# Softplus slices held back around each Silu slice, and the unit behind a Silu computed with both C products on VectorE

## The chip, the cores and the metric

The kernel runs on one NeuronCore of a Trainium2 chip. The metric is the device time of one execution in microseconds; lower is better. All arithmetic is in float32. The engines are named as the profile names them: PE is TensorE (PEld its weight load), DVE is VectorE, ACT is ScalarE, POOL is GpSimd and SP is SyncE, whose queue issues the DMAs.

## The reference, cut to what matters

The program is two residual blocks on 16 images of 64 x 64 pixels with 96 channels. The first block upsamples, applies two small matrix products with a square between them, and filters down again. The second is a state-space block (a "Mamba" block in four directions):

```
xz = x @ in_proj_w.T;  xc, z = halves of xz;  z = silu(z)
xc = silu(conv3x3_depthwise(xc) + conv_b)             # 192 channels
for each of 4 directions k:                           # rows, columns, both reversed
    dts, Bs, Cs = split(x_proj_weight[k] @ xs[k])     # 6 + 16 + 16 rows
    delta = softplus(dt_projs_weight[k] @ dts + bias)
    h[t] = exp(delta[t] * A) * h[t-1] + (delta[t] * u[t]) * B[t]   # 192 x 16 states
    y[t] = sum over the 16 states of h[t] * C[t]
y = layernorm(sum of the 4 directions) * z;  out = x + y @ out_proj_w.T
```

Each block has a group normalisation ahead of it. There are 64 x 64 = 4096 steps t for each image and direction.

## The kernel before, in words

**The scan and its units.** The scan over t dominates. It is cut into *units*: 128 partitions hold 32 channels times 4 states, and a unit covers two such groups (e = 1 and e = 0) over T = 1024 steps. For an image there are 8 *steps* (two pairs of directions, four lengths of 1024), in each step 6 blocks of channels, and in each block 4 units (j = 0 to 3, four states each). That makes 24 units in a step, 192 in an image and 3072 in all. The loop `for n, (st, bi, j) in enumerate(units)` writes out by hand the order in which every engine gets its instructions. In unit n stand, in this order:

- DVE scans group e = 1 (`recur`, lines 770 and 772, a TENSOR_TENSOR_SCAN of 128 x 1024). It reads the decay `da` (in PSUM, two buffers) and the drive `b` (in SBUF, four buffers).
- The product of h with C for e = 1 goes to POOL (line 915), or in every fifth unit (`odd_here`, SHARE = 5) to DVE (line 906). I call a unit of the second kind *odd*. In an odd unit the scan's result stays in `da`; otherwise it is written over `b`.
- `keep` (line 778) copies the last state for the next step, on DVE or, in odd units and for e = 0, on ACT.
- `decay(n + 1, 1)` (line 755) makes exp(delta * A) of the next unit on ACT. Then comes `slot(0)`.
- POOL multiplies `drive(n + 2)` (line 761, 128 x 2048).
- DVE scans e = 0, PE adds up unit n - 1 (`read_out`, line 794), then `slot(1)`; DVE multiplies with C (line 924), ACT keeps the state and makes `decay(n + 1, 0)`; every fourth unit, at j = 0, ACT copies the finished sums out (`store`, yt, line 805). Last comes `slot(2)`.

**The background work.** All else of the program is woven into those three slots of a unit. It is written as Python generators that yield after each *slice*, and `slot` lets them go on when they are due:

- `project` computes delta, delta * u, B and C for the coming step. It has 71 slices for the 72 slots of a step. For each of 6 pieces it does on ACT the softplus as Abs and Exp (lines 674, 675), Relu and Identity (677, 678), Ln and Identity (680, 681), a slice each; then PE adds the four parts in PSUM (line 686, "4 matmuls"), and three slots later DVE makes dtu (line 691) and ACT copies delta (692).
- `front` is the first block and the convolution of the next image. Its convolution has 12 tiles (8 and 4) in an image. A tile takes four slices: three with a third of the taps each on PE (line 482, the last with z_ps), and then, after `yield WAIT`, the *Silu slice*: a table load, Silu of the convolution (line 500), Silu of z (501), and the load of the usual table (502). `turn` copies the tile column-wise on ACT (line 467) and issues its stores on SP; it stands in the first slice of the next tile.
- `finish` is the end of the image before: the sum of directions, the normalisation and the output product.

`Background` counts a generator's slices against slots passed: 550 weighted slices of `front` over the 576 slots of an image, where a HEAVY slice counts twice. A slice behind `yield WAIT` goes only into slot 2. `front` and then `finish` share one place in a slot; `project` has its own. In each of the images 0 to 14 the Silu slices fall into units 99 to 128 of 192 (in the order before: 99, 102, 104, 107, 109, 112, 114, 116, 121, 123, 126, 128); the last image has no next one to prepare.

**What orders it.** Each engine takes its instructions in the order written; waits follow from the data and from the buffers' reuse. The slot's code before is this:

```
def slot(position):
    step_gen.slot(position)
    (ahead_gen if ahead_gen.gen is not None else behind_gen).slot(position)
...
odd_here = n % SHARE == SHARE - 1
```

Of the kernel before, what the change touches and what calls it, by code (L numbers as in the profile page):

```python
# [70 lines left out]
POS = 3 * 8 * 6 * NQ  # L71
SLICES = 550
WAIT = -1
HEAVY = 2
PSLICES = 71
SHARE = 5
# [3 lines left out]
def tile_two_blocks(  # L80
# [159 lines left out]
    def front(mi):  # L240
# [220 lines left out]
        for i, n, tiles, both in ((0, 128, 8, 0), (1, 64, 4, 4)):  # L461
            col = b16.tile([128, tiles * TB], F32, name="col", tag="b16")
            halves = [(n * k, t0) for k, t0 in enumerate((0, both)[:128 // n])]
            turned = None

            def turn(t, row, z):
                nc.scalar.copy(
                    col.rearrange("c (w h) -> c w h", w=HW)[:, :, 8 * t:8 * t + 8],
                    row.rearrange("c (h w) -> c w h", w=HW),
                )  # L470
                for p, t0 in halves:
                    cols = slice(TB * (t + t0), TB * (t + t0) + TB)
                    nc.sync.dma_start(out=made["xs"][2 * i, 0:n, cols], in_=row[p:p + n])
                    nc.sync.dma_start(out=made["z"][128 * i:128 * i + n, cols], in_=z[p:p + n])

            for t in range(tiles):
                c_ps = bank([128, 8, HW], "c_ps")
                for tap in range(9):
                    dy, dx = divmod(tap, 3)
                    for p, t0 in halves:  # L480
                        h0 = 8 * (t + t0) + dy
                        nc.tensor.matmul(  # L482
                            c_ps[p:p + n], lhsT=wtap_s[:, tap, 128 * i:128 * i + n],
                            rhs=xgp[:, h0:h0 + 8, dx:dx + HW], start=(tap == 0), stop=(tap == 8),
                            skip_group_check=True,
                        )
                    if tap == 2 and turned is not None:
                        turn(*turned)
                    if tap % 3 == 2 and tap < 8:
                        yield HEAVY  # L490
                z_ps = bank([128, 8, HW], "z_ps")
                for p, t0 in halves:
                    h0 = 8 * (t + t0) + 1
                    nc.tensor.matmul(
                        z_ps[p:p + n], lhsT=zwt_s[:, 128 * i:128 * i + n], rhs=xgp[:, h0:h0 + 8, 1:HW + 1],
                        start=True, stop=True, skip_group_check=True,
                    )
                yield WAIT
                row, z = piece([128, TB], "row"), piece([128, TB], "z")
                nc.scalar.activation(row, c_ps.rearrange("c h w -> c (h w)"), AF.Silu, bias=convb_s[:, i:i + 1])  # L500
                nc.scalar.activation(z, z_ps.rearrange("c h w -> c (h w)"), AF.Silu)
                nc.scalar.preload_act_table_set(BOTH)
                turned = t, row, z
                yield HEAVY
            turn(*turned)
            yield HEAVY
            if i == 0:
                yield from parts(made["xs"][1], col)
            else:
                for p, t0 in halves:  # L510
                    to = made["xs"][2, 64:128, :].rearrange("c (w h) -> c w h", h=HW)
                    for w0 in range(0, HW, 16):
                        nc.sync.dma_start(
                            out=to[:, w0:w0 + 16, 8 * t0:8 * t0 + 32],
                            in_=col[p:p + n].rearrange("c (w h) -> c w h", w=HW)[:, w0:w0 + 16, :],
                        )
                        yield HEAVY

# [96 lines left out]
    def scan():  # L615


        with ExitStack() as es:
# [14 lines left out]
            def project(mi, pair, lc, out):  # L633
# [17 lines left out]
                for t in range(0, T, TB):  # L651
                    u, ahead_u = dict(zip(order, ahead_u)), []
                    pp = gps.tile([128, TB], F32, name="pp", tag="g")
                    for v in range(3):
                        nc.tensor.matmul(pp, lhsT=xpt_s[:, pair, v, :], rhs=u[v], start=(v == 0), stop=(v == 2))
                    for _ in range(2):
                        yield
                    pr = pj.tile([128, TB], F32, name="pr")
                    nc.scalar.activation(pr, pp, AF.Identity, bias=bumps_s)


                    for i, v in enumerate(order):
                        if i == 0:
                            yield
                        s = gps.tile([128, TB], F32, name="s", tag="g")
                        nc.tensor.matmul(s, lhsT=dtw_s[:, pair, v, :], rhs=pr, start=True, stop=True)  # L666
                        if i == 0:
                            for r in range(2):
                                nc.sync.dma_start(
                                    out=rows[r, :, t:t + TB], in_=pr[64 * r:64 * r + 2 * NS, :]  # L670
                                )
                        yield
                        e, d, m, w = (pj.tile([128, TB], F32, name=k) for k in ("e", "d", "m", "w"))
                        nc.scalar.activation(e, s, AF.Abs)
                        nc.scalar.activation(e, e, AF.Exp, scale=-1.0)
                        yield
                        nc.scalar.activation(m, s, AF.Relu)
                        nc.scalar.activation(w, e, AF.Identity, bias=one_s)
                        yield
                        nc.scalar.activation(d, e, AF.Ln, bias=one_s)  # L680
                        nc.scalar.activation(w, w, AF.Identity, scale=-1.0, bias=one_s)  # L681
                        yield
                        s = gps.tile([128, TB], F32, name="s", tag="g")
                        yield
                        for k, of in enumerate((w, e, d, m)):
                            nc.tensor.matmul(s, lhsT=ident_s, rhs=of, start=(k == 0), stop=(k == 3))  # L686
                        for _ in range(3):
                            yield
                        dtu = pj.tile([128, TB], F32, name="dtu")
                        delta = pj.tile([128, TB], F32, name="delta")  # L690
                        nc.vector.tensor_mul(dtu, s, u[v])
                        nc.scalar.copy(delta, s)  # L692
                        for _ in range(2):
                            yield
                        nc.sync.dma_start(out=out["dtu"][v][:, t:t + TB], in_=dtu)
                        nc.sync.dma_start(out=out["delta"][v][:, t:t + TB], in_=delta)
                        if t + TB < T and i < 2:
                            ahead_u += [fetch_u(k, t + TB) for k in (order[:1], order[1:])[i]]
# [123 lines left out]
            class Background:  # L822

                def __init__(self, gen, slices, positions):
                    self.gen, self.slices, self.positions, self.at, self.n = gen, slices, positions, 0, 0
                    self.wait = False

                def slot(self, position):  # L830
                    self.at += 1
                    if self.wait and position < 2:
                        return
                    if self.gen is not None and self.n * self.positions < self.at * self.slices:
                        self.step()

                def step(self):
                    weight = next(self.gen, 0)
                    if weight == 0:
                        self.gen = None  # L840
                    else:
                        self.wait = weight == WAIT
                        self.n += 1 if weight in (None, WAIT) else weight

                def drain(self):
                    while self.gen is not None:
# [1 line left out]

            nothing = Background(None, 0, 1)
            ahead_gen = behind_gen = step_gen = nothing  # L850

            def slot(position):
                step_gen.slot(position)
                (ahead_gen if ahead_gen.gen is not None else behind_gen).slot(position)

            last = len(units) - 1
            def next_step(st, mi):
# [9 lines left out]
                drive(n)  # L867
            for e in range(2):
                decay(0, e)
            storing = None  # L870

            for n, (st, bi, j) in enumerate(units):
                mi, pair, lc = steps[st]
# [2 lines left out]
                if n % per_image == 0:  # L876
                    image[mi]["y"] = dram.tile([2, DI, L], F32, name="y_d")
                    behind_gen.drain()
                    ahead_gen = behind_gen = nothing
# [19 lines left out]
                    if ahead:  # L899
                        deltas[m + 1, 1] = fetch_delta(*ahead, 1)  # L900

                odd_here = n % SHARE == SHARE - 1
# [157 lines left out]
```

## Time and profile before

| what | value |
|---|---|
| median of 3 runs | 21502.07 us (21501.11 to 21510.08) |
| profiled execution, its own time | 21508.85 us |
| its span | 21507.1 us |
| DVE busy | 19512.2 us, 91% |
| POOL busy | 19511.8 us, 91% |
| PE busy | 16918.9 us, 79% |
| ACT busy | 13741.5 us, 64% |
| first scan to last scan | 536 to 21340 us |
| one image (mean of images 0 to 14) | 1304.9 us |

Times from the profile are of that one execution. A line such as "L770 DVE TENSOR_TENSOR_SCAN" names the source line, the engine and the operation; behind it stand what is written and read, how often, the busy time, the mean of one in ns, and the engine's idle time ahead of these instructions with what ended it. Where I give a figure by unit, I took the starts of the e = 1 scans (every second start of lines 770 and 772) as the units' bounds, put each instruction and the idle time just before it into the unit in which it starts, and averaged over images 0 to 14.

### The profile page before, as it was taken

The page shows a single profiled execution, that of the slowest core. Times are in us where ns is not written, and L with a number is a line of the kernel's source. Part 1 is how long each engine was busy: PE and PEld are TensorE (multiplying, and loading weights), DVE is VectorE, ACT ScalarE, POOL GpSimd, SP SyncE. Part 2 cuts the span into 40 slices and gives each one's busy share as a digit, 9 for nine tenths or more (in the row PEclk, how much of TensorE's full clock was granted, in tenths as well). Part 3 has the DMA queues.
Part 4 walks back from the last instruction along what each step waited for, and adds up shares of the span by engine and source line. Part 5 has one row for each costly group of instructions (what it writes and reads, how often), then busy time and mean ns, then how long its engine had stood idle before and what let it go on. Part 6 is the DMA issues. An engine that isn't in the chain of part 4 may idle for free. (4 is left out here: it accounts for less than half of the span.)

```text
span 21507.1 us, 273615 instructions
## 1 busy us (share of the span) xinstructions
PE 16918.9 (79%) x98988; PEld 7271.3 (34%) x98988; DVE 19512.2 (91%) x12983; ACT 13741.5 (64%) x20546; POOL 19511.8 (91%) x5538
## 2 busy tenths in 40 slices
PE   7776877878878788787878778788787888878855
PEld 4423324233332333324333242333423333243221
DVE  0999999999999999999999999999999999999997
ACT  3666666667666666666666666676666666666553
POOL 0999999999999999999999999999999999999996
PEclk8887888888889888898888888888898888888877
DMA  2565565656656566565655656566565665656654
GB/s 74 180 207 184 199 224 187 217 192 204 217 189 227 187 218 203 187 228 183 219 197 200 224 191 215 192 208 215 185 227 187 211 203 192 230 184 217 222 186 140
DMA packets 1855466, 4277.13 MB, mean 199 GB/s; under 512 B 449438, under 2 KB 548670, under 8 KB 1852062
## 3 DMA queue, kind: packets, MB, share of 16 engines
q1 hardware_dynamic: 1854110, 4259.62, 58.8%
q8 instruction: 781, 12.80, 0.2%
q14 instruction: 575, 4.71, 0.1%
HBM read 3380.58 MB, written 878.18 MB: 198 GB/s over the span
## 5 line engine op out<-in xcount | busy, mean ns | idle before, releaser
L761 POOL TENSOR_TENSOR b<-dtu,bt 128x2048 f32<-128x2048 f32 x3072 | 13905.1, 4536 | 594.2 <-DMA dtu<-dtu_d 530.5
L755 ACT ACTIVATE da<-delta,a_s 128x1024 f32<-128x1024 f32 x6144 | 6852.3, 1116 | 2859.4 <-DVE b L924 888.2
L915 POOL TENSOR_TENSOR b<-b,ct 128x1024 f32<-128x1024 f32 x2458 | 5804.1, 2361 | 1235.6 <-DVE new L778 832.6
L794 PE MATMUL y<-b,fold_s 128*32 128x256 f32 x49152 | 3837.1, 435 | 1111.6 <-DVE b L924 551.4
L924 DVE TENSOR_TENSOR b<-da,ct 128x1024 f32<-128x1024 f32 x3072 | 3756.5, 1223 | 93.9
L770 DVE TENSOR_TENSOR_SCAN da<-da,new,b 128x1024 f32<-128x1024 f32 x1383 | 3246.5, 2347 | 282.8 <-ACT da L755 274.7
L772 DVE TENSOR_TENSOR_SCAN da<-da,new,b 128x1024 f32<-128x1024 f32 x1382 | 3242.4, 2346 | 125.5 <-ACT da L755 119.1
L794 PEld LDWEIGHTS y<-b,fold_s 128*32 128x32 f32 x49152 | 1392.0, 119 | 3857.0 <-issue 1333.0
L778 ACT COPY new<-da 128x1 f32<-128x1 f32 x2764 | 434.6, 157 | 2786.4 <-DVE b L924 2294.7
L772 DVE TENSOR_TENSOR_SCAN b<-da,new,b 128x1024 f32<-128x1024 f32 x922 | 2157.9, 2341 | 47.0 <-ACT da L755 46.1
L770 DVE TENSOR_TENSOR_SCAN b<-da,new,b 128x1024 f32<-128x1024 f32 x921 | 2156.6, 2342 | 41.1 <-ACT da L755 39.5
L482 PE MATMUL c_ps<-xgp,wtap_s 96*128 96x512 f32 (+1 forms) x4608 | 1721.3, 642 | 203.6 <-ACT row L500 199.1
L686 PE MATMUL s<-w,ident_s 128*128 128x512 f32 x1536 | 1175.4, 857 | 872.0 <-ACT w L681 752.3
L666 PE MATMUL s<-pr,dtw_s 128*128 128x512 f32 x1536 | 939.0, 696 | 544.6 <-ACT delta L692 328.0
L365 PE MATMUL h_ps<-xu,w1t_s 96*128 96x500 f32 x1920 | 1059.4, 652 | 306.7 <-ACT hsq L348 124.2
L377 PE MATMUL o_ps<-w2c_s,hsq 128*100 128x96 f32 x9600 | 1031.9, 266 | 170.0 <-ACT hsq L348 143.7
L772 DVE TENSOR_TENSOR_SCAN da<-da,b 128x1024 f32<-128x1024 f32 x461 | 1055.9, 2291 | 118.4 <-ACT da L755 116.7
L770 DVE TENSOR_TENSOR_SCAN da<-da,b 128x1024 f32<-128x1024 f32 x460 | 1053.4, 2290 | 106.5 <-ACT da L755 104.3
L377 PEld LDWEIGHTS o_ps<-w2c_s,hsq 128*100 128x100 f32 x9600 | 966.1, 178 | 357.2 <-ACT hsq L348 184.9
L686 PE MATMUL s<-e,ident_s 128*128 128x512 f32 x1536 | 1022.9, 755 | 0.0
L482 PEld LDWEIGHTS c_ps<-xgp,wtap_s 96*128 96x128 f32 (+1 forms) x4608 | 600.1, 172 | 1154.9 <-issue 873.0
L787 PE MATMUL y<-y,ident_s 128*128 128x512 f32 x768 | 534.1, 784 | 538.6 <-ACT yt L805 537.1
(128 smaller groups left out, 21920.7 us busy)
## 6 DMA issues: line engine op xcount, KB each, us to landing
dtu<-dtu_d SPq DMA_DIRECT2D x1536, 512.0 KB
delta<-delta_d SPq DMA_DIRECT2D x1536, 512.0 KB
bt<-rows SPq DMA_DIRECT2D x1024, 512.0 KB
ct<-rows SPq DMA_DIRECT2D x1024, 512.0 KB
u<-xs_d SPq DMA_DIRECT2D x896, 256.0 KB
dtu_d<-dtu SPq DMA_DIRECT2D x768, 256.0 KB
delta_d<-delta SPq DMA_DIRECT2D x768, 256.0 KB
xr<-in_x SPq DMA_DIRECT2D x768, 128.0 KB
```

Source lines behind the costliest of these rows:

```text
L365: nc.tensor.matmul(h_ps[j], lhsT=w1t_s[:, 128 * j:128 * (j + 1)], rhs=xu.rearrange("c p q -> c (p q)"), start=True, stop=True,)
L377: nc.tensor.matmul(o_ps[:, p, :], lhsT=hsq[j][:, UPS * p:UPS * (p + 1)], rhs=w2c_s[:, j, :], start=(j == 0), stop=(j == HB - 1),)
L482: nc.tensor.matmul(c_ps[p:p + n], lhsT=wtap_s[:, tap, 128 * i:128 * i + n], rhs=xgp[:, h0:h0 + 8, dx:dx + HW], start=(tap == 0), stop=(tap ...
L666: nc.tensor.matmul(s, lhsT=dtw_s[:, pair, v, :], rhs=pr, start=True, stop=True)
L686: nc.tensor.matmul(s, lhsT=ident_s, rhs=of, start=(k == 0), stop=(k == 3))
L755: nc.scalar.activation(da, deltas[n // NQ, e], AF.Exp, scale=a_s[:, k, g, units[n][2]:units[n][2] + 1])
L761: nc.gpsimd.tensor_mul(b, dtus[n // NQ], bt.unsqueeze(1).to_broadcast([128, 2, T]))
L770: nc.vector.tensor_tensor_scan(out, da, b, before, ALU.mult, ALU.add)
L772: nc.vector.tensor_tensor_scan(out[:, ::-1], da[:, ::-1], b[:, ::-1], before, ALU.mult, ALU.add)
L794: nc.tensor.matmul(y[32 * q:32 * q + 32, e, :], lhsT=fold_s, rhs=b[:, e, QT * q:QT * q + QT], start=(pair == 0 and j == 0 and e == 0), sto ...
L915: nc.gpsimd.tensor_mul(h, h, bc[1, r, j])
L924: nc.vector.tensor_mul(bs[n][:, 0, :], h, bc[1, r, j])
```

## The change

A slice of `project` can now be announced as BUSY: `yield BUSY` says that the next slice is one of softplus (or the input copy pr, or dtu and delta), which load ACT. `slot` decides for both generators. When the Silu slice is due, in slot 2 and with no `store` under way (so not at j = 0), it sets `full = 2`: in this slot and the next, BUSY slices of `project` are left out. They are made up for later: where `project` lags and its slice is a light one, it may take a second light one in the same slot. The unit behind a Silu slice (`full_unit`) becomes an odd one. A running `credit` keeps the share of odd units at one in five: each odd unit takes five credits, also where it comes early, and after a run of early ones none follow until the credit is back at five. And `turn` moves from the first slice of the next tile (tap 2) to the second (tap 5).

With that, units 99 to 130 of an image get 12 or 13 odd units (6 or 7 before), and the next one comes between units 160 and 164. The numbers of instructions of each kind that compute stay the same.

```
--- before.py
+++ after.py
@@ -71,6 +71,7 @@
 POS = 3 * 8 * 6 * NQ
 SLICES = 550
 WAIT = -1
+BUSY = -2
 HEAVY = 2
 PSLICES = 71
 SHARE = 5
@@ -484,7 +485,7 @@
                             rhs=xgp[:, h0:h0 + 8, dx:dx + HW], start=(tap == 0), stop=(tap == 8),
                             skip_group_check=True,
                         )
-                    if tap == 2 and turned is not None:
+                    if tap == 5 and turned is not None:
                         turn(*turned)
                     if tap % 3 == 2 and tap < 8:
                         yield HEAVY
@@ -653,8 +654,8 @@
                     pp = gps.tile([128, TB], F32, name="pp", tag="g")
                     for v in range(3):
                         nc.tensor.matmul(pp, lhsT=xpt_s[:, pair, v, :], rhs=u[v], start=(v == 0), stop=(v == 2))
-                    for _ in range(2):
-                        yield
+                    yield
+                    yield BUSY
                     pr = pj.tile([128, TB], F32, name="pr")
                     nc.scalar.activation(pr, pp, AF.Identity, bias=bumps_s)
 
@@ -669,14 +670,14 @@
                                 nc.sync.dma_start(
                                     out=rows[r, :, t:t + TB], in_=pr[64 * r:64 * r + 2 * NS, :]
                                 )
-                        yield
+                        yield BUSY
                         e, d, m, w = (pj.tile([128, TB], F32, name=k) for k in ("e", "d", "m", "w"))
                         nc.scalar.activation(e, s, AF.Abs)
                         nc.scalar.activation(e, e, AF.Exp, scale=-1.0)
-                        yield
+                        yield BUSY
                         nc.scalar.activation(m, s, AF.Relu)
                         nc.scalar.activation(w, e, AF.Identity, bias=one_s)
-                        yield
+                        yield BUSY
                         nc.scalar.activation(d, e, AF.Ln, bias=one_s)
                         nc.scalar.activation(w, w, AF.Identity, scale=-1.0, bias=one_s)
                         yield
@@ -684,8 +685,9 @@
                         yield
                         for k, of in enumerate((w, e, d, m)):
                             nc.tensor.matmul(s, lhsT=ident_s, rhs=of, start=(k == 0), stop=(k == 3))
-                        for _ in range(3):
+                        for _ in range(2):
                             yield
+                        yield BUSY
                         dtu = pj.tile([128, TB], F32, name="dtu")
                         delta = pj.tile([128, TB], F32, name="delta")
                         nc.vector.tensor_mul(dtu, s, u[v])
@@ -823,24 +825,20 @@
 
 
 
+
                 def __init__(self, gen, slices, positions):
                     self.gen, self.slices, self.positions, self.at, self.n = gen, slices, positions, 0, 0
-                    self.wait = False
-
-                def slot(self, position):
-                    self.at += 1
-                    if self.wait and position < 2:
-                        return
-                    if self.gen is not None and self.n * self.positions < self.at * self.slices:
-                        self.step()
+                    self.said = None
+
+                def due(self):
+                    return self.gen is not None and self.n * self.positions < self.at * self.slices
 
                 def step(self):
-                    weight = next(self.gen, 0)
-                    if weight == 0:
+                    self.said = next(self.gen, 0)
+                    if self.said == 0:
                         self.gen = None
                     else:
-                        self.wait = weight == WAIT
-                        self.n += 1 if weight in (None, WAIT) else weight
+                        self.n += self.said if self.said is not None and self.said > 0 else 1
 
                 def drain(self):
                     while self.gen is not None:
@@ -848,10 +846,25 @@
 
             nothing = Background(None, 0, 1)
             ahead_gen = behind_gen = step_gen = nothing
+            full, full_unit = 0, None
 
             def slot(position):
-                step_gen.slot(position)
-                (ahead_gen if ahead_gen.gen is not None else behind_gen).slot(position)
+                nonlocal full, full_unit
+                back = ahead_gen if ahead_gen.gen is not None else behind_gen
+                back.at += 1
+                step_gen.at += 1
+                gate = back.said == WAIT and back.due() and position == 2 and storing is None
+                if gate:
+                    full, full_unit = 2, n + 1
+                if step_gen.due() and not (full and step_gen.said == BUSY):
+                    light = step_gen.said != BUSY
+                    step_gen.step()
+
+                    if light and step_gen.due() and step_gen.said != BUSY:
+                        step_gen.step()
+                if back.due() and (gate or back.said != WAIT):
+                    back.step()
+                full = max(full - 1, 0)
 
             last = len(units) - 1
             def next_step(st, mi):
@@ -867,7 +880,7 @@
                 drive(n)
             for e in range(2):
                 decay(0, e)
-            storing = None
+            storing, credit = None, 0
 
             for n, (st, bi, j) in enumerate(units):
                 mi, pair, lc = steps[st]
@@ -899,7 +912,11 @@
                     if ahead:
                         deltas[m + 1, 1] = fetch_delta(*ahead, 1)
 
-                odd_here = n % SHARE == SHARE - 1
+
+                credit += 1
+                odd_here = n == full_unit or credit >= SHARE
+                if odd_here:
+                    credit -= SHARE
                 h = das[n, 1] if odd_here else bs[n][:, 1, :]
                 recur(n, 1, h)
                 if odd_here:
```

More of the change, by code (lines that the diff above doesn't have):

```diff
@@ L73 @@
 WAIT = -1
+BUSY = -2
 HEAVY = 2
@@ L486, in front @@
                         )
-                    if tap == 2 and turned is not None:
+                    if tap == 5 and turned is not None:
                         turn(*turned)
@@ L655, in project @@
                         nc.tensor.matmul(pp, lhsT=xpt_s[:, pair, v, :], rhs=u[v], start=(v == 0), stop=(v == 2))
-                    for _ in range(2):
-                        yield
+                    yield
+                    yield BUSY
                     pr = pj.tile([128, TB], F32, name="pr")
@@ L671, in project @@
                                 )
-                        yield
+                        yield BUSY
                         e, d, m, w = (pj.tile([128, TB], F32, name=k) for k in ("e", "d", "m", "w"))
@@ L675, in project @@
                         nc.scalar.activation(e, e, AF.Exp, scale=-1.0)
-                        yield
+                        yield BUSY
                         nc.scalar.activation(m, s, AF.Relu)
                         nc.scalar.activation(w, e, AF.Identity, bias=one_s)
-                        yield
+                        yield BUSY
                         nc.scalar.activation(d, e, AF.Ln, bias=one_s)
@@ L686, in project @@
                             nc.tensor.matmul(s, lhsT=ident_s, rhs=of, start=(k == 0), stop=(k == 3))
-                        for _ in range(3):
+                        for _ in range(2):
                             yield
+                        yield BUSY
                         dtu = pj.tile([128, TB], F32, name="dtu")
@@ L827, in __init__, with due @@
                     self.gen, self.slices, self.positions, self.at, self.n = gen, slices, positions, 0, 0
[L828 to L835, printed above, removed]
+                    self.said = None
+                def due(self):
+                    return self.gen is not None and self.n * self.positions < self.at * self.slices
                 def step(self):
-                    weight = next(self.gen, 0)
-                    if weight == 0:
+                    self.said = next(self.gen, 0)
+                    if self.said == 0:
                         self.gen = None
                     else:
-                        self.wait = weight == WAIT
-                        self.n += 1 if weight in (None, WAIT) else weight
+                        self.n += self.said if self.said is not None and self.said > 0 else 1
                 def drain(self):
@@ L850, in scan @@
             ahead_gen = behind_gen = step_gen = nothing
+            full, full_unit = 0, None
             def slot(position):
-                step_gen.slot(position)
-                (ahead_gen if ahead_gen.gen is not None else behind_gen).slot(position)
+                nonlocal full, full_unit
+                back = ahead_gen if ahead_gen.gen is not None else behind_gen
+                back.at += 1
+                step_gen.at += 1
+                gate = back.said == WAIT and back.due() and position == 2 and storing is None
+                if gate:
+                    full, full_unit = 2, n + 1
+                if step_gen.due() and not (full and step_gen.said == BUSY):
+                    light = step_gen.said != BUSY
+                    step_gen.step()
+                    if light and step_gen.due() and step_gen.said != BUSY:
+                        step_gen.step()
+                if back.due() and (gate or back.said != WAIT):
+                    back.step()
+                full = max(full - 1, 0)
             last = len(units) - 1
@@ L869, in scan @@
                 decay(0, e)
-            storing = None
+            storing, credit = None, 0
             for n, (st, bi, j) in enumerate(units):
@@ L900, in scan @@
                         deltas[m + 1, 1] = fetch_delta(*ahead, 1)
-                odd_here = n % SHARE == SHARE - 1
+                credit += 1
+                odd_here = n == full_unit or credit >= SHARE
+                if odd_here:
+                    credit -= SHARE
                 h = das[n, 1] if odd_here else bs[n][:, 1, :]
```

## The prediction

> **What bounds the kernel now.** I read the page's busy totals first, then the groups, then busy time by stretch, then the waits of the worst stretch, last its timeline.
>
> ```profile
> PE 16918.9 (79%) x98988; PEld 7271.3 (34%) x98988; DVE 19512.2 (91%) x12983; ACT 13741.5 (64%) x20546; POOL 19511.8 (91%) x5538
> ```
>
> VectorE (DVE) and GpSimd (POOL) are equally busy; ScalarE (ACT) is not the bound on average. The groups that set the two:
>
> ```profile
> L761 POOL TENSOR_TENSOR b<-dtu,bt 128x2048 f32<-128x2048 f32 x3072 | 13905.1, 4536 | 594.2 <-DMA dtu<-dtu_d 530.5
> ...
> L915 POOL TENSOR_TENSOR b<-b,ct 128x1024 f32<-128x1024 f32 x2458 | 5804.1, 2361 | 1235.6 <-DVE new L778 832.6
> ...
> L924 DVE TENSOR_TENSOR b<-da,ct 128x1024 f32<-128x1024 f32 x3072 | 3756.5, 1223 | 93.9
> ```
>
> I call a unit odd when VectorE takes both products with C. Per unit POOL does 4.54 us (L761), and 2.36 (L915) unless odd; back to back the starts of two L761 stand 6.80 apart (POOL's timeline, 10682.65 to 10696.25, two pairs). DVE does two scans (2.3 each), L924 (1.22), a small copy; an odd unit adds L906 (1.225) and drops the copy (0.155): **+1.07 us**. So five units need about 32 us of either.
>
> A unit starts at its first scan, so the starts of L770/L772 cut each image into 192 units. Image 7 of 0 to 15: units 0-98, 99-130 (the Silu stretch), 131-163, 164-191, and for comparison 99-130 of image 15, which has no next image to prepare:
>
> ```profile
> 9664.80:10343.20 678.40, 512.68 (x3778) 264.43 (x3778) 631.55 (x411) 449.74 (x721) 630.82 (x180) 0.83 0.56 190
> 10343.20:10572.10 228.90, 200.31 (x934) 74.39 (x934) 200.01 (x138) 172.47 (x233) 205.17 (x58) 0.93 0.59 204
> 10572.10:10793.20 221.10, 184.41 (x792) 61.41 (x796) 214.19 (x155) 128.63 (x196) 209.49 (x61) 0.89 0.71 231
> 10793.20:10972.70 179.50, 143.58 (x686) 47.84 (x686) 178.17 (x112) 105.88 (x138) 174.78 (x51) 0.91 0.68 228
> 20753.50:20957.90 204.40, 124.04 (x626) 41.88 (x618) 198.88 (x137) 115.73 (x171) 204.40 (x59) 0.74 0.53 189
> ```
>
> Columns: length, then PE, PEld, DVE, ACT, POOL busy. In the Silu stretch DVE idles 228.9 - 200.0 = 29 us; without the background work the same units take 204.4. Afterwards (third row) DVE idles 7. The Silu stretch's waits:
>
> ```profile
> DVE da L772 <- ACT da L755: 12.0, 9, 4.0
> DVE b L772 <- ACT da L755: 9.1, 5, 3.3
> DVE dtu L691 <- PE s L686: 4.0, 2, 3.0
> ```
>
> DVE waits for the decays that ACT makes (L755), and for matmuls whose inputs ACT made late. The worst place:
>
> ```profile
> 10444.62 0.59 ACT L677 ACTIVATE m<-s 128x512 f32<-128x512 f32 x1
> 10445.10 0.72 ACT L678 ACTIVATE w<-e,one_s 128x512 f32<-128x512 f32 x1
> 10445.84 1.28 ACT L500 ACT_TABLE_LOAD   x1
> 10447.13 0.69 ACT L500 ACTIVATE row<-c_ps,convb_s 128x512 f32<-128x512 f32 x1
> 10447.72 0.59 ACT L501 ACTIVATE z<-z_ps 128x512 f32<-128x512 f32 x1
> 10448.33 1.28 ACT L502 ACT_TABLE_LOAD   x1
> 10449.62 1.12 ACT L755 ACTIVATE da<-delta,a_s 128x1024 f32<-128x1024 f32 x1
> ```
>
> A Silu slice holds ACT 3.78 us (10445.84 to 10449.62). Here a softplus slice stands ahead of it and another (L680, L681) behind; DVE's scan at 10450.84 had waited 3.05, the next 1.00, and the late 4-matmul sum cost dtu 3.02 more.
>
> **What the Trainium skill says.** "ScalarE: Activation LUTs", What ACT_TABLE_LOAD costs: a load takes about 1283 ns, and some 1380 ns of drain. The trace has 1283 for each; of a drain nothing shows, the next instruction starts at once, so I use 3.78 us for the slice. "SBUF - State Buffer", Who interferes with whom: a DVE instruction with at most one SBUF input doesn't contend with GpSimd. L906 reads da from PSUM; L761 keeps 4482 to 4653 ns in the whole trace, which agrees, so I charge a moved product nothing for contention.
>
> **The change part by part.** The orders that the two sources give differ in units 100 to 163 of images 0 to 14 alone; image 15 and the rest keep theirs. Each image has 12 Silu slices, 180 in all.
>
> *Odd units behind a Silu.* Units 99-130 hold 96 odd units in 15 images before, 183 after: 5.8 more per image. Units 131-163 hold 12 instead of 99. No product is added. Price in the Silu stretch: 5.8 x 1.07 = 6.2 us of DVE work. But 3 of 15 images already have an odd unit right behind any given Silu, since 192 is not a multiple of 5. Over the 12 Silus, the two units behind have 20.7 us of DVE idle where the first is odd and 30.0 where no odd unit is near; the spans of three units sum to 258.7 and 255.8. Twelve odd units that should cost 12.8 cost 3.0: the product lies in the stall.
>
> *Softplus slices withheld and Silu moved.* Withheld are those in the Silu's own slot and the next one. The Silu no longer goes at j = 0, where yt's copy (0.58) is: those of units 104, 112, 116 and 128 go one unit later, and 114's with them, to 115. Of the four that wait for the convolution's matmuls (L500 on PE, 9.4 us in image 7: after 99, 104, 123, 128), two get a unit more. The work is only postponed; it costs nothing where ACT has room (it is busy 172 of 229 us).
>
> *turn at tap 5.* The copy L467 (1.09) and its two or four stores go one slice later, out of the slot right behind the Silu, into one where they may stand with a softplus slice (2.3 together). On SP the stores pass conv slices that issue nothing; I count 0 there, cover: nothing reads them before the image's end.
>
> *Two light steps in one slot.* Catching up shortens the way from the four matmuls (L686, 5.1 us on PE) to dtu (L691) from three slots to two, twice per image (units 110 and 131). Not seen before; bounds 0 (PE free) and 3.0 (the worst above); I take 2 each.
>
> DVE's stalls per image in 99-130, averaged over 15 images, before -> my estimate after: Silu 99 3.9 -> 3.0 (PE still late); 104 1.9 -> 0.9; 107 0.9 and dtu 0.4 -> 1.4; 109 4.6 -> 2.5; 112 8.1 -> 0.9; 114 and 116 1.0 -> 0.6; 121 1.9 -> 0.5; 123 2.8 -> 2.1; 128 1.6 -> 0.9; unattached 1.5 -> 1.5. About 28.5 -> 14.3, so -14; I book -13.4, as neighbouring stalls overlap. With +6.2 of moved work: **-7.2 per image, -108 in 15**.
>
> *The price behind it.* From 131 on there is no odd unit for some 30 units. DVE alone would then be faster by 6.6 - 0.8 = 5.8 odd units, but POOL must do both products: from the first scan of 131 to that of 164 it needs 2.35 + 32 x 6.80 = 220 us, plus early waits before DVE is ahead (0.9 at 131, 2 at dtu in 132): 223, against 221.5 now. +1.5 in 14 images; image 0, which has no finish work beside it, takes 209.9 now, so +11. **+32 in all.** Later units keep their odd ones; POOL idles 4.7 of 179.5 us there, which takes up its lag.
>
> Sum: -108 + 32 = -76 against the profiled execution's 21508.85, or 21433. It stood 7 above the median 21502.07, so 21426; I say **21425**.
>
> **Rivals.** About 43 us (0.2%) is what a measurement of this kernel can tell from no change.
> *Moved stalls, no gain (0.22).* Postponed slices collide with the next decays: Silu to Silu is only 2.4 units, ACT's stalls fall by 8, not 13. For it: ACT 75% busy there, turn beside Abs and Exp. Then -8 + 6.2 + 2.1 = +0.3 per image: 21506.
> *POOL becomes the bound, slower (0.22).* Its place is units 131-163: 33 pairs x 6.80 + 2.35 = 227 if POOL also waits for each early DVE stall, +5.5 per image. It decides once the Silu stretch gains under 5.5; with 2 gained, +3.5 x 15 = 53: 21555. Against it: POOL is waiting, not late, when 131 starts, and DVE has about 0.3 us per unit to build a lead.
> *All stalls at Silus go (inside my 0.56 for faster).* Then 99-130 takes 204.4 + 6.2 + 4 = 214.6, -14.5 x 15 = -218 with 32 given back: 21316.
> That the change does nothing is excluded: the order does move.
>
> **How the numbers follow.** Faster 0.56 (the forecast and the last case), same 0.22, slower 0.22. Range 21310 to 21560: the full gain to the POOL case; it holds the bound 0 to 3 of dtu (15 x 6 = 90).
>
> **What would show it.** Right: stretch 99-130 near 222 with DVE idle near 16; 131-163 near 223 with POOL busy almost throughout; L755's waits of DVE halved there. Wrong: that stretch at 229 or more with new stalls at 106, 111 or 132, or 131-163 beyond 225. L761, L906 and L915 should keep counts and durations.

## The result, and the profile after

The changed kernel takes **21417.59 us** (median of 7 runs, 21416.18 to 21430.62), against 21502.41 before (7 runs). The ratio is 0.9962, 95% interval 0.995 to 0.9973: faster by 85 us. The forecast was 21425.

Its profiled execution has a span of 21415.5 us. The totals by engine and the groups that set them, from its page and its groups (the lines are now L763, L932, L941 and L923 for L761, L915, L924 and L906):

```profile
PE 16916.2 (79%) x98988; PEld 7258.4 (34%) x98988; DVE 19508.0 (91%) x12983; ACT 13744.9 (64%) x20546; POOL 19513.1 (91%) x5538
```

```profile
L763 POOL TENSOR_TENSOR b<-dtu,bt 128x2048 f32<-128x2048 f32 x3072 | 13905.1, 4535 | 620.3 <-DMA dtu<-dtu_d 538.5 <-PE y L796 74.8 <-issue 5.0
...
L932 POOL TENSOR_TENSOR b<-b,ct 128x1024 f32<-128x1024 f32 x2458 | 5801.5, 2360 | 1115.7 <-DVE new L780 748.6 <-issue 228.2 <-DVE b L772 50.4
...
L941 DVE TENSOR_TENSOR b<-da,ct 128x1024 f32<-128x1024 f32 x3072 | 3757.1, 1223 | 93.4
...
L923 DVE TENSOR_TENSOR b<-da,ct 128x1024 f32<-128x1024 f32 x614 | 752.0, 1225 | 45.4 <-DVE da L774 0.9 <-issue 0.4
```

Counts, durations and busy sums are those of before. Nothing got faster or rarer; only idle time went. Busy time by stretch shows where: image 7, units 0-98, 99-130, 131-163 and 164-191 (length, then PE, PEld, DVE, ACT and POOL busy):

```profile
9638.70:10317.40 678.70, 519.44 (x3778) 266.50 (x3778) 631.67 (x412) 449.78 (x721) 631.07 (x180) 0.82 0.56 189
10317.40:10536.10 218.70, 195.73 (x934) 73.35 (x934) 204.43 (x137) 169.72 (x232) 192.74 (x53) 0.96 0.63 215
10536.10:10760.90 224.80, 186.06 (x792) 61.21 (x796) 210.05 (x155) 131.35 (x197) 221.28 (x66) 0.88 0.69 224
10760.90:10940.40 179.50, 143.59 (x687) 47.86 (x686) 178.17 (x111) 105.88 (x138) 175.42 (x51) 0.91 0.68 230
```

In the Silu stretch (second row) 228.9 us became 218.7 although DVE works 4.4 us more: its idle time fell from 29 to 14. In the next stretch DVE works 4 us less and POOL 12 us more, and 221.1 became 224.8. POOL is busy for 98% of it. The waits of DVE, first in the Silu stretch, then in the one behind it (in the last fence the only line of before):

```profile
DVE b L774 <- ACT da L757: 6.9, 3, 3.5
DVE da L774 <- ACT da L757: 3.7, 4, 1.0
DVE dtu L693 <- PE s L687: 0.6, 2, 0.3
DVE b L923 <- DVE da L774: 0.5, 1, 0.5
```

```profile
DVE da L774 <- ACT da L757: 5.8, 7, 1.1
DVE b L774 <- POOL b L763: 4.0, 8, 0.7
DVE dtu L693 <- DMA ct<-rows: 2.6, 1, 2.6
```

```profile
DVE da L772 <- ACT da L755: 4.8, 6, 1.1
```

The waits for decays in the Silu stretch halved (21.1 to 10.6) and those for the four matmuls nearly went (4.0 to 0.6). Behind it, where decays had been DVE's only waits (4.8), two are new: for POOL's drive (L763), and one of 2.6 at dtu of unit 132, which this view puts down to a DMA as the last to come; e5 will show that it is the way from the four matmuls. The Silu slice of the worst place of before now stands one unit later, in unit 114. There ACT does this:

```profile
10420.44 1.12 ACT L757 ACTIVATE da<-delta,a_s 128x1024 f32<-128x1024 f32 x1
10421.57 1.28 ACT L501 ACT_TABLE_LOAD   x1
10422.87 0.69 ACT L501 ACTIVATE row<-c_ps,convb_s 128x512 f32<-128x512 f32 x1
10423.45 0.59 ACT L502 ACTIVATE z<-z_ps 128x512 f32<-128x512 f32 x1
10424.06 1.28 ACT L503 ACT_TABLE_LOAD   x1
10425.35 0.16 ACT L780 COPY new<-da 128x1 f32<-128x1 f32 x1
10425.55 1.12 ACT L757 ACTIVATE da<-delta,a_s 128x1024 f32<-128x1024 f32 x1
```

and on DVE:

```profile
10422.38 1.23 DVE L923 TENSOR_TENSOR b<-da,ct 128x1024 f32<-128x1024 f32 x1
10423.52 2.29 DVE L774 TENSOR_TENSOR_SCAN da<-da,b 128x1024 f32<-128x1024 f32 x1
10425.84 1.22 DVE L941 TENSOR_TENSOR b<-da,ct 128x1024 f32<-128x1024 f32 x1
10426.99 0.68 DVE L693 TENSOR_TENSOR dtu<-s,u 128x512 f32<-128x512 f32 x1
10427.58 2.28 DVE L774 TENSOR_TENSOR_SCAN b<-da,b 128x1024 f32<-128x1024 f32 x1
```

No softplus slice stands directly at the Silu, the odd product (L923) lies beside it, and the decay is done at 10426.67, ahead of the scan at 10427.58.

Averages over images 0 to 14 are used from here on, by units as before. The four stretches together give the time of one image. Each row is one profiled execution. No edit on shared buffers (before to e5, and e7) touches units 0-98, and yet they take 673.9 to 675.7 there: that is the scatter. The executions of e2 and e11 were 15 us faster and 21 us slower than the medians of their kernels, so their rows are off by about a microsecond per image.

| kernel | 0-98 | 99-130 | 131-163 | 164-191 | DVE idle in 99-130 |
|---|---|---|---|---|---|
| before | 675.7 | 229.4 | 220.8 | 179.0 | 29.9 |
| changed | 675.0 | 219.2 | 225.1 | 178.9 | 14.5 |
| e1: slices only | 674.7 | 218.5 | 224.2 | 179.3 | 19.1 |
| e2: odd units only | 673.9 | 225.5 | 222.5 | 178.9 | 20.0 |
| e3: turn at tap 2 | 674.8 | 222.0 | 225.2 | 178.9 | 16.9 |
| e4: none withheld | 674.2 | 222.3 | 222.7 | 178.9 | 16.7 |
| e5: three slots to dtu | 675.7 | 219.2 | 222.8 | 179.0 | 14.6 |
| e6: own buffers | 654.2 | 217.2 | 223.5 | 180.1 | 12.6 |
| e7: Silu later | 675.2 | 222.4 | 224.8 | 179.3 | 15.5 |
| e8: e1, e5, e6, e7 | 653.6 | 220.7 | 218.0 | 179.0 | 20.1 |
| e9: e5, e6 | 652.3 | 217.4 | 221.2 | 178.9 | 12.8 |
| e10: e1, e5, e6 | 653.2 | 214.6 | 217.7 | 179.1 | 15.4 |
| e11: before, own buffers | 653.7 | 220.3 | 216.5 | 179.1 | 21.2 |

### The profile page after: what moved, and what is told of

Its sections match the earlier page's. It is cut to its first block, busy times and chain, and to the rows that moved or that the text cites. A ratio compares the mean times of both kernels' runs of the same rounds, so it can differ in the third digit from the quotient of the medians.

```text
span 21415.5 us, 273671 instructions
## 1 busy us (share of the span) xinstructions
PE 16916.2 (79%) x98988; PEld 7258.4 (34%) x98988; DVE 19508.0 (91%) x12983; ACT 13744.9 (64%) x20546; POOL 19513.1 (91%) x5538
## 5 line engine op out<-in xcount | busy, mean ns | idle before, releaser
L763 POOL TENSOR_TENSOR b<-dtu,bt 128x2048 f32<-128x2048 f32 x3072 | 13905.1, 4535 | 620.3 <-DMA dtu<-dtu_d 538.5
L932 POOL TENSOR_TENSOR b<-b,ct 128x1024 f32<-128x1024 f32 x2458 | 5801.5, 2360 | 1115.7 <-DVE new L780 748.6
L941 DVE TENSOR_TENSOR b<-da,ct 128x1024 f32<-128x1024 f32 x3072 | 3757.1, 1223 | 93.4
L772 DVE TENSOR_TENSOR_SCAN da<-da,new,b 128x1024 f32<-128x1024 f32 x1383 | 3246.5, 2347 | 281.5 <-ACT da L757 272.7
L774 DVE TENSOR_TENSOR_SCAN da<-da,new,b 128x1024 f32<-128x1024 f32 x1322 | 3101.5, 2346 | 101.0 <-ACT da L757 93.7
L774 DVE TENSOR_TENSOR_SCAN b<-da,new,b 128x1024 f32<-128x1024 f32 x982 | 2299.8, 2342 | 126.9 <-POOL b L763 68.1
L772 DVE TENSOR_TENSOR_SCAN b<-da,new,b 128x1024 f32<-128x1024 f32 x921 | 2156.6, 2342 | 40.5 <-ACT da L757 38.3
L483 PE MATMUL c_ps<-xgp,wtap_s 96*128 96x512 f32 (+1 forms) x4608 | 1628.3, 608 | 99.4 <-ACT row L501 94.9
L774 DVE TENSOR_TENSOR_SCAN da<-da,b 128x1024 f32<-128x1024 f32 x521 | 1192.6, 2289 | 61.1 <-ACT da L757 59.4
L772 DVE TENSOR_TENSOR_SCAN da<-da,b 128x1024 f32<-128x1024 f32 x460 | 1053.5, 2290 | 108.3 <-ACT da L757 105.9
L687 PE MATMUL s<-d,ident_s 128*128 128x512 f32 x1536 | 923.4, 687 | 0.0
```

The costliest lines, as they stand in the source:

```text
L483: nc.tensor.matmul(c_ps[p:p + n], lhsT=wtap_s[:, tap, 128 * i:128 * i + n], rhs=xgp[:, h0:h0 + 8, dx:dx + HW], start=(tap == 0), stop=(tap ...
L763: nc.gpsimd.tensor_mul(b, dtus[n // NQ], bt.unsqueeze(1).to_broadcast([128, 2, T]))
L772: nc.vector.tensor_tensor_scan(out, da, b, before, ALU.mult, ALU.add)
L774: nc.vector.tensor_tensor_scan(out[:, ::-1], da[:, ::-1], b[:, ::-1], before, ALU.mult, ALU.add)
L932: nc.gpsimd.tensor_mul(h, h, bc[1, r, j])
L941: nc.vector.tensor_mul(bs[n][:, 0, :], h, bc[1, r, j])
```

## The experiments

**e1, the slices without the odd units.**

```
-odd_here = n == full_unit or credit >= SHARE
+odd_here = n % SHARE == SHARE - 1
```

> The changed kernel with the odd units back at every fifth place (0 credit), all else of the change kept. Theory A (stalls are relieved mainly by holding softplus back and by taking the Silu out of j = 0; the odd unit only lets its own product lie in a stall): stretch 99-130 near 220 us per image against 219.2 in the changed kernel and 229.4 before, stretch 131-163 near 224 (221 as before, plus the new dtu stall of 2.7 at unit 132), so the whole 60 to 110 us under the kernel before. Rival B (the odd unit behind the Silu is what removes the stalls): 99-130 at 226 or more, the whole within 40 us of the kernel before.

Measured: 21387.96 us (ratio to before 0.9947, 0.9932 to 0.9962). The Silu stretch takes 218.5, no more than in the changed kernel: theory A, and the whole, 117 under the kernel before, gains a little more than A's 60 to 110. The moved slices alone carry the gain. DVE idles 19.1 us instead of 14.5, but has 5.8 odd products per image less to do there. Note the stretch behind: it takes 224.2, 3.4 more than before, although no odd unit came early and none is paid back. DVE waits 2.76 us at dtu of unit 132 (0.08 before), and POOL idles 0.37 us per unit, so POOL is not what makes it longer.

**e2, the odd units without the slices.** In the kernel before, `full_unit` is set when the Silu slice goes, and the odd units follow the credit:

```
+if back.wait and position == 2 and back.n * back.positions < (back.at + 1) * back.slices:
+    full_unit = n + 1
...
-odd_here = n % SHARE == SHARE - 1
+credit += 1
+odd_here = n == full_unit or credit >= SHARE
+if odd_here:
+    credit -= SHARE
```

> The kernel before with only the odd units placed behind the Silu slices and paid back later; slices, turn and Silu where they were before. Theory A: the 5.8 extra odd units per image lie in stalls, 99-130 near 228.5 us (229.4 before), 131-163 near 223 because GpSimd is the bound there, so the whole 0 to 45 us slower than before, about 21520. Rival B: 99-130 near 221, the whole 60 us or more faster than before.

Measured: 21466.82 us (0.9982, 0.9974 to 0.999). Neither theory has it right. It is faster than before, where I had it slower, but by far not enough for B: the Silu stretch gains 3.9, and the stretch behind loses 1.7. There POOL does not idle at all (0.00 us per unit, 0.31 before): POOL is the bound, and the payment falls mostly on image 0 (209.9 to 220.7; 221.5 to 222.6 in the others). So each part relieves stalls on its own (3.9 by the odd units, 10.9 by the slices), and together they give 10.2: in part they relieve the same ones. By unit, DVE's idle time at 106, 111, 118 and 130 (1.90, 3.69, 0.95 and 1.60 before) falls with the slices alone (0.08, 1.80, 0.08, 0.08) and with the odd units alone (0.53, 1.25, 0.14, 0.28). The longest, at 114 (7.17), goes with the slices (0.13) and stays with the odd units (6.81).

**e3, turn back in the first slice.**

```
-if tap == 5 and turned is not None:
+if tap == 2 and turned is not None:
```

> The changed kernel with turn back in the first slice behind the Silu (tap 2). Theory A: the copy of 1.09 us stands in slot 0 instead of slot 1 or 2 of the unit behind; both slots lie ahead of the same decay, so 99-130 within 2 us of 219.2 and the whole within 30 us of the changed kernel, rather above it. Rival C (the slot right behind the Silu is the one that matters): about 0.7 us more at each of 12 Silus, +8 per image, the whole 21540.

Measured: 21459.4 us (0.998, 0.9972 to 0.9988), 42 above the changed kernel (the two intervals just touch). The Silu stretch is 2.8 longer and so outside A's 2, but far from C's 8. Most of it stands at three places, where DVE idles 1.88 instead of 0.66 (unit 111), 1.07 instead of 0.07 (123), and 1.33 instead of 0.79 (121); at 125 it idles 0.5 less. In the forecast I had booked nothing for turn.

**e4, nothing withheld.**

```
-full, full_unit = 2, n + 1
+full, full_unit = 0, n + 1
```

> The changed kernel with no softplus slice withheld (so no catching up either): odd units, the rule against j = 0 and turn at tap 5 stay. Theory A: the stalls at units 107, 111, 123 and 130/131 come back in part, 99-130 near 224 us; dtu keeps its three slots, so the 2.7 us at unit 132 vanish and 131-163 is near 222; the whole 21440 to 21480. Rival D (withholding does nothing, the moved Silu does it all): 99-130 at 219 to 220 and, with the dtu stall gone, the whole 30 us or more under the changed kernel.

Measured: 21418.48 us (0.9961, 0.9946 to 0.9976), the same as the changed kernel. The stretches, 222.3 and 222.7, are nearer to A than to D. Withholding saves 3.1 us per image at the Silus (2.64 at 107 here, 1.07 in the changed kernel) and gives 2.4 back in the stretch behind, where DVE idles 0.07 here and 3.18 there at unit 132, though 2.44 here and 1.07 there at 131. That these two cancel is why the whole doesn't move: on these buffers, the slices that are held back pay nothing in the end. Of the 10.9 of the moved slices, withholding and turn (2.8 by e3) account for about a half, if they add up; the Silu kept off j = 0, which all of e1, e3 and e4 have, was not run alone. In all three the wait at unit 114 is gone (0.14 at most). The total is lower than A's since 99-130 is 1.7 shorter than it said, and the first stretch, which no part of the change touches, 0.8 shorter than in the changed kernel.

**e5, three slots to dtu.** A second light step is not taken behind the four matmuls:

```
 for _ in range(2):
-    yield
+    yield ALONE
 yield BUSY
...
-if light and step_gen.due() and step_gen.said != BUSY:
+if light and step_gen.due() and step_gen.said not in (BUSY, ALONE):
```

> The changed kernel, but a second light step in a slot is not taken between the four matmuls and dtu, so that dtu keeps three slots. Theory A: the stall of 3.2 us at unit 132 (two slots in the changed kernel, 0.1 where three) goes; VectorE has no lead there yet, so it counts in full: stretch 131-163 from 225.1 to about 222.4 us, the whole about 40 us under the changed kernel (21376). Rival E (TensorE is late anyway, or GpSimd, the bound of that stretch, eats the gain): the wait moves to dtu one slot later or into waits for the drive, 131-163 stays above 224, the whole within 15 us of the changed kernel.

Measured: 21389.31 us (0.9948, 0.9933 to 0.9963). DVE's idle time in unit 132 falls from 3.18 to 0.97 and 131-163 from 225.1 to 222.8: theory A, though a third of the wait stays. The whole is 28 lower where A had 40, and the intervals overlap, so the stretch is what shows it. The shortened way from matmuls to dtu is the cost of catching up.

**e6, own buffers of da.**

```
-aps = es.enter_context(tc.tile_pool(name="sc_aps", bufs=2, space=PSUM))
+aps = es.enter_context(tc.tile_pool(name="sc_aps", bufs=1, space=PSUM))
...
-da = aps.tile([128, T], F32, name="da")
+da = aps.tile([128, T], F32, name="da", tag=f"da{e}")
```

> The changed kernel with one fixed PSUM buffer of da for e = 1 and one for e = 0, in place of two that are shared by turns; the same space, the same order. In the changed kernel's built order 465 decays for e = 0 are given the buffer that the unit's own first scan still reads, so they wait for it; at units 107, 113 and 131 of each image stands a stall of 1.0 us of this form. Theory F: these stalls go everywhere, 465 x 0.9 = 420 us, less what lies beside GpSimd's bound: 21000 to 21200; 99-130 near 216. Rival G (the stall comes from ScalarE being late, the buffer only follows): less than 60 us, and the three stalls stay.

Measured: 21049.82 us (0.9791, 0.9776 to 0.9805), 368 below the changed kernel: theory F. Most lies in units 0-98 (20.8 per image), which the change doesn't touch. One such place, unit 51 of image 7 in the kernel before:

```profile
10019.36 2.34 DVE L770 TENSOR_TENSOR_SCAN b<-da,new,b 128x1024 f32<-128x1024 f32 x1
10021.74 1.12 ACT L755 ACTIVATE da<-delta,a_s 128x1024 f32<-128x1024 f32 x1 [1.50 <-DVE b L770]
10022.89 2.36 DVE L770 TENSOR_TENSOR_SCAN da<-da,new,b 128x1024 f32<-128x1024 f32 x1 [1.00 <-ACT da L755]
```

ACT is not late here: it has idled 1.50 us until the unit's first scan was through with the buffer, then makes the decay, and the second scan waits 1.00 for it. Over the whole traces, second scans that wait more than 0.5 us behind a decay which starts within 0.12 us of the end of the unit's first scan number 365 in the kernel before (366 us in all) and 357 in the changed one (359 us, beside the 368 won); with own buffers (this run) there are 5. At the Silus the own buffers give 2.0: the stall at 107 falls from 1.07 to 0.55, at 113 to 0.58, at 131 to 0.37, at 101 from 2.99 to 0.74; but 108, 111 and 120 to 121 get 2.6 us more together.

**e7, Silu not right behind its matmuls.** `since` is the slot in which the WAIT was announced:

```
-gate = back.said == WAIT and back.due() and position == 2 and storing is None
+gate = back.said == WAIT and back.due() and position == 2 and storing is None and back.at - back.since > 1
```

> The changed kernel, but a Silu slice may not follow the convolution's last matmuls in the very next slot; the Silus of units 99 and 123 go to 101 and 125 (some that follow shift by a unit). Theory A: the stalls of 3.0 and 3.5 us at units 101 and 125 are ScalarE waiting for TensorE in front of Silu; they fall under 0.7 each and 99-130 takes about 214 us (219.2), the whole about 75 us under the changed kernel (21343). Rival H (the stall is the Silu's own length): it moves to 102 and 126, 99-130 stays at 218 or more.

Measured: 21460.59 us (0.9981, 0.9974 to 0.9989), 43 slower than the changed kernel; both are missed. The two stalls do go (2.99 and 3.54 to 0.07 each). But the late start has to be made up: Silus then stand in 101, 103, 105 and again 125, 127, 129, two units apart, and DVE idles 0.88 at 106, 2.69 at 107, 1.68 at 111 and 2.53 at 131. So in this run the room behind each Silu was worth more than a Silu that doesn't wait.

**e8, all of it.** The edits of e1, e5, e6 and e7 on the changed kernel.

> All together on the changed kernel: odd units at every fifth place, three slots to dtu, Silu not in the slot right behind its matmuls, own buffers of da. Theory: the gains of the single runs add up as far as they lie in different units: 30 + 40 + 75 + 420 less some overlap, 20850 to 21050. If VectorE's stalls were hidden behind GpSimd, it stays above 21200.

Measured: 20995.55 us (0.9766, 0.9751 to 0.978). In the range, but with e7 in it; e10 shows what that costs.

**e9, own buffers and three slots** (e5 and e6 together).

> The changed kernel with own buffers of da and three slots to dtu. The three-slot rule took 28 us off the changed kernel; if that adds to the own buffers (21050), 21020. If VectorE, now with fewer stalls, runs into GpSimd in stretch 131-163, nothing is added: 21050.

Measured: 20988.03 us (0.9761, 0.9746 to 0.9776). It adds 62, more than 28: 2.3 per image in 131-163, and 1.9 and 1.2 in 0-98 and 164-191, where these edits change no order against e6, so a part is scatter. DVE's waits in 131-163, image 7:

```profile
DVE b L775 <- POOL b L764: 6.8, 14, 0.8
DVE da L775 <- ACT da L758: 1.5, 2, 1.2
DVE dtu L694 <- PE s L688: 0.4, 1, 0.4
```

With most of ACT's stalls gone, what is left is POOL: 14 waits for the drive, and POOL idles 0.03 us per unit. This is the payment for the early odd units.

**e10, the same with odd units at every fifth place** (e1, e5 and e6).

> As the former, with the odd units back at every fifth place. Theory A (the odd unit behind a Silu and the moved slices remove the same stalls, and paying back costs in 131-163 where GpSimd is the bound): stretch 131-163 near 218 instead of 221, 99-130 within 1 us of it, the whole 20 to 50 us under it, 20980, and below all others. If the odd unit still fills a stall here, it is slower than the former.

Measured: **20909.09 us** (0.9725, 0.9709 to 0.9742), 79 below e9, more than the 20 to 50 of theory A, and the fastest kernel here. 131-163 takes 217.7 instead of 221.2, and the Silu stretch 214.6 instead of 217.4. DVE's waits in 131-163 without the payment:

```profile
DVE da L775 <- ACT da L758: 1.5, 2, 1.2
DVE dtu L694 <- PE s L688: 0.7, 2, 0.5
```

The waits for POOL are gone. Against e8 it lacks only e7's rule: 220.7 became 214.6 at the Silus.

**e11, the kernel before with own buffers.**

> The kernel before with only the own buffers of da. 477 decays of it have the shared form, against 465 of the changed kernel, so it should win the same 370 us: 21130, and the change keeps its worth of 80 us on top. If the stalls at the Silus hide behind the buffers' ones, the difference to the changed kernel with own buffers (21050) shrinks under 40.

Measured: 20961.14 us (0.9751, 0.9737 to 0.9766). The first expectation is missed: own buffers take 541 off the kernel before, not 370. The second points the right way, but the difference to e6 doesn't just shrink, it turns round. This kernel is 89 **below** e6, so on own buffers the change as it stands makes the kernel slower. (Of the 541, the 366 of the waits under e6 are traced to their instructions; the rest is not.) Its gain at the Silus shrinks from 10.2 to 3.1 (220.3 to 217.2), and its price in 131-163 grows from 4.3 to 7.0 (216.5 to 223.5), while DVE in the kernel before hardly waits there any more:

```profile
DVE da L772 <- ACT da L755: 1.3, 1, 1.3
```

is its only wait in that stretch.

## Why the prediction was right, and where its steps were off

**The total** was 21425 against 21417.6, and the rivals' numbers (21506, 21555, 21316) are all further off.

**The Silu stretch.** Forecast -7.2 per image to some 222 with 16 us idle; measured -10.2, to 219.2 with 14.5 idle. The terms that I mis-sized: the stall at Silu 109 and the dtu behind it (2.5 booked; 0.07 and 0.66 measured at 110 and 111); those at 104, 121 and 128 (2.3 booked together; 0.35 measured at 106, 123 and 130); and turn, worth 2.8 by e3, booked at nothing (1.2 of it lies at unit 111 and 1.0 at 123, so it is in part the same time). The stall at Silu 123 grew (2.8 to 3.5, booked 2.1).

**The price behind it.** Forecast +1.5 in 14 images, 223; measured 225.1 there, +3.6. Image 0: +11 forecast, 209.9 to 224.4 measured. The forecast had POOL as the bound of the whole stretch, with DVE's early waits on top. e1 and e2 part the two: the slices alone cost 3.4 in this stretch, mostly at dtu of unit 132 (2.76; 3.18 in the changed kernel, 2 booked), and the odd units alone 1.7, with POOL as the bound and +10.8 in image 0, as forecast. Together they cost 4.3, less than their sum, as with the gain. The dtu wait was the term that was too small.

**The sum.** 15 x -10.2 = -153 and 15 x 4.3 = +64 make -89, beside -92 in span. Forecast were -108 and +32. Two errors of some 45 and 32 us in opposite directions made the total look better than its terms: that it came within 8 us is luck. (The sum for the last rival is slightly off too: from 229.4 to 214.6 is 14.8, not 14.5.)

**The step that failed** is the odd unit's part: "the product lies in the stall". In the kernel before that is so. e2 shows it: 6.2 us more of DVE's work there take 9.9 us off its idle time. But the forecast has one table of stalls for both parts and never asks what the slices alone leave. e1 answers: with the slices moved, 4.6 of the 6.2 us still lie in idle time (19.1 to 14.5), but they shorten nothing, as the stretch takes 218.5 without the odd units and 219.2 with them. Behind it the price comes on top: 0.9 us per image against e1, and 3.5 on own buffers with the dtu wait eased (e9 against e10).

**What I did not see** is that a part of the stalls was of another kind. In the built order 477 decays of the kernel before, and 465 of the changed one, are given the PSUM buffer which the same unit's first scan still reads; in the Silu stretch of images 0 to 14, 81 and 42 of them. The forecast read their 1.0 us as ACT being late; the traces under e6, and e6 and e11 themselves, show that it was the buffers. The halving from 81 to 42 came with the new order and was not intended (the slices alone leave 48). A part of the change's gain is therefore probably of this kind: on own buffers the slices take the Silu stretch from 220.3 (e11) to 214.6 (e10, with e5's rule), 5.7 instead of 10.9.

**The forecast's other marks.** For it: L763, L923 and L932 keep counts and durations, POOL is busy almost throughout 131-163, DVE's waits for the decays in the Silu stretch are halved, and units 0-98 and 164-191 keep their times to within 0.7 us. Against it: 131-163 went beyond 225, if only just (225.1), which I had named as a sign of being wrong. What it stands for, a dearer payment than booked, did come. The new stall at unit 132 came as well, but the Silu stretch stayed far below the 229 that was to go with it. Whether e1 is faster than the changed kernel (by 30) stays open for the whole time, as the intervals overlap.

## What to carry to other kernels

Two remedies for the same stall don't add up: put each alone and both together beside the original before keeping both, and price what each takes elsewhere. Work borrowed by one of two balanced engines is paid back where the other is the bound; here that cost 3.5 us per image once other stalls were gone. Work that is only postponed can cost too, where it has to be made up for: the shortened way to dtu took back most of what holding softplus back had gained. And before slices are moved about a stall, look which buffer the waiting instruction was given; a fixed buffer for each use was worth four times as much as the whole reordering (368 against 85 us).

## What the runs showed of the hardware

A product on DVE with one input in PSUM and one in SBUF cost POOL nothing that shows: in the kernel before, the 763 drives (L761) that ran beside such a product (L906) took 4537 ns in the mean and the other 2309 took 4535; in the changed kernel it is 4534 (758 of L763 beside L923) and 4535 (2314). After the second table load of a Silu slice the next instruction starts at once (10424.06 plus 1.28 is 10425.34, the start 10425.35), here as before.
